# A Mamba block and a mixture of experts on one core: delta's arithmetic moved to 128 partitions by transfers instead of PE transposes, the W_x products and the choosing moved within a round, every table computed in parts

## The chip, the core and the metric

The kernel runs on one core of a Trainium2 chip, in float32 throughout (a few small counting products are bfloat16). The engines of the core have a queue each and run side by side: TensorE (PE) multiplies matrices into PSUM, VectorE (DVE) and ScalarE (ACT) do elementwise work, GpSimd (POOL) does a little of that and issues the indirect transfers (gathers and scatters by a list of rows), and SyncE (SP) issues the other transfers. The metric is the device time of one execution in microseconds, the median over several runs.

## The reference

Two layers, each with a residual sum and a layernorm behind it. T = 4096 tokens of D = 256 values.

```python
xz = x @ W_in                                   # [T, 1024]
conv_in, gated = xz[:, :512], xz[:, 512:]
convolved = silu(causal_conv_of_4_taps(conv_in) + conv_b)
x_dbl = convolved @ W_x                         # [T, 33]
delta = softplus(x_dbl[:, :1])                  # one value per token
Bm, Cm = x_dbl[:, 1:17], x_dbl[:, 17:]
deltaA  = exp(delta * -exp(A_log))              # [T, 16]
deltaBx = delta * Bm * convolved[:, :16]
h_t = deltaA_t * h_(t-1) + deltaBx_t            # along the 4096 tokens
ssm = sum over the 16 states of h_t * Cm_t      # one value per token
x = layernorm(x + ((ssm + convolved * D_param) * silu(gated)) @ W_out)

expert = argmax(x @ Wr.T + br)                  # 8 experts, one per token
y = relu(x @ W1[expert].T + b1[expert]) @ W2[expert].T + b2[expert]
out = layernorm(x + y)
```

## The kernel before

**Two layers in one stream.** The first layer goes in 8 chunks of 512 tokens; its channels lie on partitions and its tokens along the free axis, so that the recurrence over tokens is one scan instruction of DVE. The second layer goes in 32 blocks of 128 tokens of one expert each. A block's rows are gathered from a table in DRAM (`x1d`), into which the first layer scatters its rows by expert. The 2.2 MB of an expert's weights are gathered by POOL into one of three buffers. A block is four *quarters* of PE work: two of `hidden` (lines 617, 626, 628) and two of `close` (line 642).

**What sets the order.** PE's order is exactly that in which the program emits its products. The other engines' orders come from a scheduler, which takes a step marked `@urgent` first. The program emits in rounds: the string `ROUND` lists the steps of a round, each as `name.part:behind`, and in round r the step works on chunk r - behind. So the round with chunk r's projection holds the W_x product of chunk r - 1 (`gauge:1`), its scan (`scan:1`), the gating and output projection of chunk r - 2 (`gate:2`, `project_out:2`), and the ranks of chunk r - 3. `QUARTERS` tells, for each round, how many expert quarters follow each entry; before, they begin in round 7 and the rounds are 12. The quarters left over follow after the last round.

**The steps of a chunk.**
- `project.c` (line 781): two products of 128x512 for each of eight columns of tiles, c = 0 to 3 for the convolution, 4 to 7 for the gate. ACT evicts (796, 798, 800) from three PSUM banks, and takes the silu of a convolved tile (807).
- `taps.c` (752): the three other taps of the convolution, on DVE.
- `gauge` (823): the W_x product with two halves of the channels on two halves of the partitions; ACT copies the result (`pxs`, 828).
- `gauge_out`: four PE transposes (837) bring tokens onto partitions, four tokens to a partition. ACT copies, DVE adds the two halves (`xd`, 847), and the softplus is computed in some fifteen small operations on 128x4 (852 to 871). The result goes into `sr`, delta repeated for 16 states.
- `scan`: four PE transposes (884) bring `sr` back with states on partitions. ACT takes the exponential (886), DVE multiplies (888), scans (890), multiplies by C (896) and splits the product into bfloat16 parts (899).
- `gate`: PE sums over states (`py`, 914), DVE adds the skip and multiplies by the gate (916, 920; one of four tiles on POOL, except in the last two chunks).
- `project_out` (961) multiplies by W_out, with router columns beside it; DVE adds the residual (965), ACT takes squares (968) and normalises (984). `look` and `look_out` (932, 946) give the router's share of x itself.
- `choose` (1000 to 1012) finds each token's expert, `rank` (1022 to 1041) its place, and scatters the rows. `blocks_of` runs `table()`, a generator of small DVE steps that says which rows and weights each block has: early tables after chunks 2, 4 and 5 for 5, 13 and 17 blocks, a final one after the last chunk. Before, an early table is emitted in one piece; the final one is stepped once per quarter. Then `prefetch` issues gathers of rows (532) and weights (561).

SP issues, at the start of a round, the load of the next chunk's x transposed (`xTb`) and of its rows (`xb`), 512 KB each. The constant weights are issued in round 0 by `load_later`. Twelve transposes into an unused bank (229) run at the start, ahead of the first data.

Of the kernel before, what the change touches and what calls it, by code (L numbers as in the profile page):

```python
# [30 lines left out]

# [6 lines left out]
F32 = mybir.dt.float32  # L38
# [8 lines left out]
P = 128  # L47
# [17 lines left out]
WARM = 12  # L65
# [4 lines left out]
SLOTS = 3  # L70
RUN = -(-(SURE - EARLY[6]) // SLOTS)

# [26 lines left out]
RD, RB, RC = 0, 32, 64  # L99
NR = RC + NS  # L100


ROUND = """
    project.0:0 gauge:1 gate:2 project.1:0 taps.0:0 gauge_out:1 taps.1:0 project.2:0
    project.3:0 taps.2:0 project_out.0:2 taps.3:0 rank:3 project_out.1:2 project_out.2:2
    blocks_of:3 look_weights:0 project.4:0 project.5:0 look_out:1 project.6:0 scan:1
    project_out.3:2 choose:2 look:0 project.7:0
"""
ROUNDS = 12

QUARTERS = {
    7: "03001202020010100010001000",
    8: "00100000010110110000000021",
    9: "10001011000101000000001001",
    10: "00000000000110000110000222",
    11: "00010000000000000000000000",
# [6 lines left out]
def mamba_moe(  # L123
# [34 lines left out]
    st = {}  # L158

# [50 lines left out]
    def load_later():  # L210

        nc.sync.dma_start(wx[:, :, 0:XW], W_x.rearrange("(c p) n -> p c n", p=P))
# [15 lines left out]
    for n in range(WARM):  # L228
        nc.tensor.transpose(idle[:, n % 4 * P : (n % 4 + 1) * P], ident, ident)
# [30 lines left out]

    sr = const.tile([P, JT, NR], F32, name="sr")
    nc.gpsimd.memset(sr, 0.0)
# [552 lines left out]
    @urgent  # L815
    def gauge(i):
# [10 lines left out]
        s_["pxs"] = a2.tile([P, TB], F32, tag="pxs", name=f"pxs{i}", bufs=1)  # L827
        nc.scalar.copy(s_["pxs"], px)

    @urgent  # L830
    def gauge_out(i):

        s_ = st[i]
        px = bank("tr", f"pxo{i}", 2)
        for j in range(JT):
            at = slice(j * P, (j + 1) * P)
            nc.tensor.transpose(px[:, at], s_["pxs"][:, at], ident)
        pxv = px.rearrange("p (j h n) -> p j h n", h=P // H, n=H)

        def by_state(a):  # L840
            return a.unsqueeze(2).to_broadcast([P, JT, NS])

        xd = a2.tile([P, JT, XW], F32, tag="xd", name=f"xd{i}", bufs=1)

        parts = a2.tile([P, JT, 2, XW], F32, tag="parts", name=f"parts{i}", bufs=1)
        nc.scalar.copy(parts, pxv[:, :, :, 0:XW])
        nc.vector.tensor_tensor(xd, parts[:, :, 0, :], parts[:, :, 1, :], ALU.add)
        nc.scalar.copy(sr[:, :, RC : RC + NS], xd[:, :, 1 + NS : XW])
        x0 = xd[:, :, 0]

# [300 lines left out]
```

## Time and profile before

| | us |
|---|---|
| median of 3 runs (lowest to highest) | 464.55 (464.51 to 464.59) |
| the profiled execution's own time | 467.2 |
| its span | 465.4 |
| PE busy in the span | 453.4 |
| DVE, ACT, POOL busy | 312.3, 234.4, 159.3 |
| one steady chunk (of rounds 2 to 4) | 25.2 |
| 264 products of the projection (line 781) | 119.0 |
| 864 and 432 products of the expert blocks without extra rows (617, 642) | 102.2, 99.4 |
| 256 products by W_out (961) | 61.9 |
| 64 W_x products (823) | 15.5 |

A profile shows one execution. Times are microseconds (us) within its span. The page's busy times count matmuls with ends that are modelled, so that neighbours overlap: of two groups of products, the difference of their starts tells the cost. In the list of costly groups, `out<-in` are the program's names of the tiles, followed by the shape, the count, the busy time and the mean of one in ns; behind the last bar stands the idle time of the engine just before them, with what ended it. The list of waits names an engine's instruction, the one that released it, and the total, the count and the longest of these waits. In the table of windows the columns are the stretch, its length, each engine's busy time with its instructions in brackets, the granted PE clock, the share of the DMA engines and GB/s. In the timeline a row has the start, the length, the engine and the instruction. In the list of transfers the last number is the median from issue to landing.

### The profile page before, as it was taken

To read this page: it belongs to the slowest core of one execution; us is meant where nothing else is said; L and a number is where in the kernel's file an instruction comes from. 1 tells how busy PE (TensorE), PEld (TensorE's weight loads), DVE (VectorE), ACT (ScalarE), POOL (GpSimd) and SP (SyncE) were. 2 spreads that over 40 slices of the span, in tenths; PEclk is the share of its full clock that TensorE was granted. 3 is DMA by queue.
4 is the path that set the end of the run, shared out by engine and by line. 5 is a ranking of instruction groups with operands and counts; after the bars stand their busy time and mean duration, and the time that the engine had idled before them with its cause. 6 is when DMAs were issued, how large, how long until landed. Compare 5 with 4: busy or idle time off the path is not lost. (4 is left out here: it accounts for less than half of the span.)

```text
span 465.4 us, 7267 instructions
## 1 busy us (share of the span) xinstructions
PE 453.4 (97%) x2496; PEld 339.9 (73%) x2496; DVE 312.3 (67%) x1002; ACT 234.4 (50%) x510; POOL 159.3 (34%) x184
## 2 busy tenths in 40 slices
PE   8999999999999999999999998999999999999994
PEld 6344646465554667876898888999989898989983
DVE  1687969797989869846969368645556565645452
ACT  4787898989879895758553421121212121212120
POOL 3001003214155402352242654435454454434311
PEclk9999999999999999999999999999999999999999
DMA  7501011211229811925646869889986298667400
GB/s 236 176 4 46 0 46 48 89 48 49 92 64 389 353 54 41 365 85 217 247 170 255 283 201 317 328 341 393 360 326 223 58 326 326 227 242 266 179 17 24
DMA packets 20040, 87.38 MB, mean 188 GB/s; under 512 B 4978, under 2 KB 10877, under 8 KB 16418
## 3 DMA queue, kind: packets, MB, share of 16 engines
q0 software_dynamic: 9616, 76.32, 44.2%
q1 hardware_dynamic: 9426, 10.31, 6.7%
q10 hardware_dynamic: 960, 0.27, 0.3%
q8 instruction: 20, 0.33, 0.3%
q14 instruction: 18, 0.15, 0.1%
HBM read 87.16 MB, written 8.77 MB: 206 GB/s over the span
## 5 line engine op out<-in xcount | busy, mean ns | idle before, releaser
L781 PE MATMUL pm<-xTb,win 128*128 128x512 f32 (+1 forms) x264 | 119.0, 589 | 0.0
L617 PEld LDWEIGHTS ph<-xgT,we 128*128 128x128 f32 x864 | 100.4, 192 | 5.4 <-issue 1.8
L617 PE MATMUL ph<-xgT,we 128*128 128x128 f32 x864 | 102.2, 276 | 0.2 <-issue 0.2
L642 PE MATMUL pe<-we,hT 128*128 128x256 f32 x432 | 99.4, 380 | 1.6 <-DVE hT L628 1.2
L642 PEld LDWEIGHTS pe<-we,hT 128*128 128x128 f32 x432 | 79.4, 190 | 13.3 <-DVE hT L628 2.6
L781 PEld LDWEIGHTS pm<-xTb,win 128*128 128x128 f32 x264 | 48.4, 193 | 47.7 <-issue 43.6
L752 DVE SCALAR_TENSOR_TENSOR acc<-xc,cw,acc 128x512 f32<-128x512 f32 x96 | 70.3, 744 | 15.4 <-DMA wx<-in_W_x 8.0
L284 ACT ACTIVATE sdm<-mvm,eps 128x1 f32<-128x1 f32 x32 | 9.4, 294 | 129.9 <-DVE mvm L282 113.1
L961 PE MATMUL po<-wout,sg 128*128 128x265 f32 x256 | 61.9, 389 | 0.7 <-DVE sg L920 0.7
L961 PEld LDWEIGHTS po<-wout,sg 128*128 128x128 f32 x256 | 47.2, 190 | 11.1 <-issue 2.4
L532 POOL DMA_INDIRECT xg<-x1d,tidx x32 | 31.7, 989 | 61.2 <-DMA out<-y,xg 45.6
L561 POOL DMA_INDIRECT we<-in_experts,widx x32 | 34.1, 1064 | 47.7 <-DVE xg L666 10.8
L682 POOL DMA_INDIRECT out<-y,xg x32 | 33.6, 1050 | 42.2 <-DVE y L286 25.5
L628 DVE TENSOR_SCALAR hT<-ph,we 128x128 f32<-128x128 f32 x108 | 31.2, 344 | 24.9 <-PE ph L617 14.9
L1041 POOL DMA_INDIRECT x1d<-x,at x32 | 34.7, 1083 | 29.1 <-DVE q L867 7.4
L666 DVE TENSOR_TENSOR xg<-pe,xg 128x256 f32<-128x256 f32 x32 | 13.5, 423 | 41.9 <-PE pe L642 39.3
L626 ACT ACTIVATE hT<-ph,we 128x128 f32<-128x128 f32 x108 | 30.8, 367 | 13.1 <-PE ph L617 6.7
L965 DVE TENSOR_TENSOR xb<-po,xb 128x265 f32<-128x265 f32 x32 | 13.7, 430 | 26.7 <-PE po L961 25.4
L920 POOL TENSOR_TENSOR sg<-cv,sg 128x512 f32<-128x512 f32 x6 | 7.7, 1278 | 60.4 <-DVE cv L916 60.4
L798 ACT COPY xc<-pm 128x512 f32<-128x512 f32 x32 | 18.6, 581 | 15.4 <-PE pm L781 15.4
L800 ACT ACTIVATE acc<-pm,cb,cw 128x512 f32<-128x512 f32 x32 | 25.1, 784 | 0.2
L968 ACT ACTIVATE x<-xb 128x256 f32<-128x256 f32 x32 | 16.1, 504 | 16.3 <-DVE xb L965 11.9
(221 smaller groups left out, 579.0 us busy)
## 6 DMA issues: line engine op xcount, KB each, us to landing
xb<-in_x SPq DMA_DIRECT2D x8, 512.0 KB, 3.3
xTb<-in_xT SPq DMA_DIRECT2D x7, 512.0 KB, 3.4
win<-in_W_in SPq DMA_DIRECT2D x1, 512.0 KB, 5.9
we<-in_W_outT SPq DMA_DIRECT2D x1, 512.0 KB, 6.1
wout<-in_W_out SPq DMA_DIRECT2D x1, 512.0 KB, 7.0
x1d<-x,at POOLq DMA_INDIRECT x32
we<-in_experts,widx POOLq DMA_INDIRECT x32
xg<-x1d,tidx POOLq DMA_INDIRECT x32
```

Of the source, the lines that this page charges most:

```text
L532: read = nc.gpsimd.indirect_dma_start(out=to.bitcast(I32), out_offset=None, in_=x1d, in_offset=bass.IndirectOffsetOnAxis(ap=at, axis=0),)
L561: nc.gpsimd.indirect_dma_start(out=wes[n][:, :], out_offset=None, in_=experts, in_offset=bass.IndirectOffsetOnAxis(ap=weights[n], axis=0), ...
L617: nc.tensor.matmul(ph[:, n * w : (n + 1) * w], lhsT=we[:, at : at + P], rhs=xgT[:, dc * w : (dc + 1) * w], start=(dc == 0), stop=(dc == DC ...
L626: nc.scalar.activation(hT[:, fc, :], ph[:, n * w : (n + 1) * w], AF.Relu, bias=bias)
L628: last[b] = nc.vector.tensor_scalar(hT[:, fc, :], ph[:, n * w : (n + 1) * w], bias, 0.0, ALU.add, ALU.max)
L642: nc.tensor.matmul(py[:, 0:D], lhsT=hT[:, fc, 0:P], rhs=out_weights(fc), start=(fc == 0), stop=(fc == FC - 1),)
L682: moved = nc.gpsimd.indirect_dma_start(out=out, out_offset=bass.IndirectOffsetOnAxis(ap=at, axis=0), in_=rows, in_offset=None, bounds_chec ...
L752: nc.vector.scalar_tensor_tensor(acc, xc[:, c, k : k + TB], cw[:, c, k : k + 1], acc, ALU.mult, ALU.add)
L781: nc.tensor.matmul(banks[c][:, at], lhsT=win[:, dc, c * P : (c + 1) * P], rhs=xTb[:, dc, at], start=(dc == 0), stop=(dc == DC - 1),)
L800: evicted = nc.scalar.activation(acc, pm, AF.Identity, scale=cw[:, c, KC - 1 : KC], bias=cb[:, c : c + 1])
L961: nc.tensor.matmul(po[:, 0 : D + NM], lhsT=sg[:, c, j * P : (j + 1) * P], rhs=wout[:, c, :], start=(c == 0), stop=(c == CC - 1),)
L1041: moved = nc.gpsimd.indirect_dma_start(out=x1d, out_offset=bass.IndirectOffsetOnAxis(ap=at[:, j : j + 1], axis=0), in_=x1s[i % X1S][:, j, ...
```

## The change

- *Delta.* The two groups of four transposes go. The columns of W_x are laid out anew, B first, then delta's column repeated 16 times, then C; this takes three transfers and a copy on DVE. `gauge` adds the two halves on DVE (`half`, `bcd`), which leaves 16 equal rows of 512 pre-activations on partitions 16 to 31, and a transfer brings these 16x512 onto 128 partitions by 64 (`x0`). The new step `delta` does the softplus there, on 128x64 instead of 128x4, and a second transfer brings it back to 16x512 (`wide`). `scan` works from these without PE.
- *Order of a round.* `gauge` moves from the next round's start to the end of the chunk's own, `look` to the next round, `delta` and `scan` follow; `choose` is listed just before `gauge`. `gauge`, `scan`, `look_out`, `rank` and `blocks_of` lose their mark `@urgent`; `delta` has one.
- *Tables.* Early tables become generators that are stepped once per entry of a round, with the prefetch at their end; the final one starts 8 quarters later.
- *The rest.* `gate`'s last tile of the last two chunks goes to POOL. The warm-up is 8 float32 products on a constant that DVE sets, instead of 12 transposes. The quarters are placed anew, from round 6 on, and the rounds are 17.

```diff
...
 
 
 from contextlib import ExitStack
+from itertools import chain
 
 import concourse.bass as bass
 import concourse.tile as tile
...
 
 SURE = 32
 
-WARM = 12
+WARM = 8
 
 AHEAD = 2
 
 
 SLOTS = 3
+
+WAIT = 8
 RUN = -(-(SURE - EARLY[6]) // SLOTS)
...
 OC = OB + FC
 WROW = OC + D
 
-RD, RB, RC = 0, 32, 64
+RB, RD, RC = 0, 16, 32
 NR = RC + NS
+SEG = P // NS
 
 
 ROUND = """
-    project.0:0 gauge:1 gate:2 project.1:0 taps.0:0 gauge_out:1 taps.1:0 project.2:0
-    project.3:0 taps.2:0 project_out.0:2 taps.3:0 rank:3 project_out.1:2 project_out.2:2
-    blocks_of:3 look_weights:0 project.4:0 project.5:0 look_out:1 project.6:0 scan:1
-    project_out.3:2 choose:2 look:0 project.7:0
+    project.0:0 gate:2 taps.0:0 look:1 look_weights:0 project.1:0 project.2:0 taps.2:0
+    taps.1:0 project_out.0:2 project.3:0 project_out.1:2 taps.3:0 look_out:1 project.4:0
+    rank:3 delta:1 project.5:0 project_out.2:2 project.6:0 blocks_of:3 scan:1
+    project_out.3:2 choose:2 gauge:0 project.7:0
 """
-ROUNDS = 12
+ROUNDS = 17
 
 QUARTERS = {
-    7: "03001202020010100010001000",
-    8: "00100000010110110000000021",
-    9: "10001011000101000000001001",
-    10: "00000000000110000110000222",
-    11: "00010000000000000000000000",
+    6: "00000000000000000001001001",
+    7: "00201001000001100000000230",
+    8: "20110002001000000000000010",
+    9: "12001000000100100300001010",
+    10: "00000010001100000000001000",
+    12: "00011010000000010000000000",
+    16: "00000001000000000000000000",
 }
 
 LOG_SERIES = (0.33333338, 0.19999444, 0.14308298, 0.1071537, 0.1214478)
...
 
     st = {}
 
+    stir = const.tile([P, P], F32, name="stir")
+    nc.vector.memset(stir, 1.0)
+
     def load(i):
 
         xTb = a2.tile([P, DC, TB], F32, tag="xTb", name=f"xTb{i}")
...
 
     def load_later():
 
-        nc.sync.dma_start(wx[:, :, 0:XW], W_x.rearrange("(c p) n -> p c n", p=P))
+        for to, n, at in ((RB, NS, 1), (RC, NS, 1 + NS), (NR, 1, 0)):
+            nc.sync.dma_start(
+                wx[:, :, to : to + n], W_x[:, at : at + n].rearrange("(c p) n -> p c n", p=P)
+            )
+        nc.vector.tensor_copy(
+            wx[:, :, RD : RD + NS], wx[:, :, NR : NR + 1].to_broadcast([P, CC, NS])
+        )
         nc.sync.dma_start(al, A_log)
         nc.sync.dma_start(dp, D_param)
         nc.sync.dma_start(woutT, W_outT.rearrange("(c p) n -> p c n", p=P))
...
 
     idle = bank("tr", "idle", 2)
     for n in range(WARM):
-        nc.tensor.transpose(idle[:, n % 4 * P : (n % 4 + 1) * P], ident, ident)
+        nc.tensor.matmul(
+            idle[:, n % 4 * P : (n % 4 + 1) * P], lhsT=stir, rhs=stir, start=True, stop=True
+        )
 
     def iota(shape, pattern, base, channel, name, dtype=F32):
         t = const.tile(shape, dtype, name=name)
...
         trib, oneb, pattern=[[1, P]], compare_op=ALU.is_gt, fill=0.0, base=0,
         channel_multiplier=-1,
     )
-
-    sr = const.tile([P, JT, NR], F32, name="sr")
-    nc.gpsimd.memset(sr, 0.0)
 
     parts_ = const.tile([P, TB], F32, name="parts_")
     nc.gpsimd.memset(parts_, 0.0)
...
             )
             nc.gpsimd.tensor_copy(after[:, :, 0 : KC - 1], xc[:, :, TB : TB + KC - 1])
 
-    @urgent
     def gauge(i):
...
                 px[g : g + H, :], lhsT=wx[:, c, :], rhs=cv[:, c, :],
                 start=(c < 2), stop=(c >= CC - 2), tile_position=(0, g),
             )
-        s_["pxs"] = a2.tile([P, TB], F32, tag="pxs", name=f"pxs{i}", bufs=1)
-        nc.scalar.copy(s_["pxs"], px)
+        half = a2.tile([P, TB], F32, tag="half", name=f"half{i}", bufs=1)[0:NR, :]
+        nc.scalar.copy(half, px[H : H + NR, :])
+        bcd = s_["bcd"] = a2.tile([P, TB], F32, tag="bcd", name=f"bcd{i}", bufs=2)
+        nc.vector.tensor_tensor(bcd[0:NR, :], px[0:NR, :], half, ALU.add)
+        x0 = s_["x0"] = a2.tile([P, TB // SEG], F32, tag="x0", name=f"x0{i}")
+        nc.sync.dma_start(x0, bcd[RD : RD + NS, :])
 
     @urgent
-    def gauge_out(i):
-
-        s_ = st[i]
-        px = bank("tr", f"pxo{i}", 2)
-        for j in range(JT):
-            at = slice(j * P, (j + 1) * P)
-            nc.tensor.transpose(px[:, at], s_["pxs"][:, at], ident)
-        pxv = px.rearrange("p (j h n) -> p j h n", h=P // H, n=H)
-
-        def by_state(a):
-            return a.unsqueeze(2).to_broadcast([P, JT, NS])
-
-        xd = a2.tile([P, JT, XW], F32, tag="xd", name=f"xd{i}", bufs=1)
-
-        parts = a2.tile([P, JT, 2, XW], F32, tag="parts", name=f"parts{i}", bufs=1)
-        nc.scalar.copy(parts, pxv[:, :, :, 0:XW])
-        nc.vector.tensor_tensor(xd, parts[:, :, 0, :], parts[:, :, 1, :], ALU.add)
-        nc.scalar.copy(sr[:, :, RC : RC + NS], xd[:, :, 1 + NS : XW])
-        x0 = xd[:, :, 0]
-
-        e = a2.tile([P, JT], F32, tag="e", name=f"e{i}")
+    def delta(i):
+
+        x0 = st[i]["x0"]
+
+        def small(tag):
+            return a2.tile([P, TB // SEG], F32, tag=tag, name=f"{tag}{i}", bufs=1)
+
+        e = small("e")
         nc.vector.scalar_tensor_tensor(e, x0, -1.0, x0, ALU.mult, ALU.min)
         grown = nc.scalar.activation(e, e, AF.Exp)
         if i == 0:
             with tc.issue_after(grown.ins):
                 nc.scalar.activation(nega, al, AF.Exp)
             nc.vector.tensor_scalar(nega, nega, -1.0, None, ALU.mult)
-        s = a2.tile([P, JT], F32, tag="s", name=f"s{i}")
+        s = small("s")
         nc.vector.tensor_scalar(s, e, 2.0, None, ALU.add)
         nc.vector.reciprocal(s, s)
         nc.vector.tensor_tensor(s, s, e, ALU.mult)
-        w = a2.tile([P, JT], F32, tag="w", name=f"w{i}")
+        w = small("w")
         nc.vector.tensor_tensor(w, s, s, ALU.mult)
-        q = a2.tile([P, JT], F32, tag="q", name=f"q{i}")
+        q = small("q")
         nc.vector.tensor_scalar(q, w, LOG_SERIES[-1], None, ALU.mult)
         for a in LOG_SERIES[-2::-1]:
             nc.vector.scalar_tensor_tensor(q, q, a, w, ALU.add, ALU.mult)
         nc.vector.scalar_tensor_tensor(q, q, 1.0, s, ALU.add, ALU.mult)
-        delta = a2.tile([P, JT], F32, tag="delta", name=f"delta{i}")
-        nc.vector.tensor_scalar(delta, x0, 0.0, None, ALU.max)
-        nc.vector.scalar_tensor_tensor(
-            sr[:, :, RD : RD + NS], by_state(q), 2.0, by_state(delta), ALU.mult, ALU.add
-        )
-        nc.vector.tensor_tensor(
-            sr[:, :, RB : RB + NS], xd[:, :, 1 : 1 + NS], sr[:, :, RD : RD + NS], ALU.mult
-        )
-
-    @urgent
+        nc.vector.tensor_scalar(x0, x0, 0.0, None, ALU.max)
+        nc.vector.scalar_tensor_tensor(q, q, 2.0, x0, ALU.mult, ALU.add)
+        wide = st[i]["wide"] = a2.tile([P, TB], F32, tag="wide", name=f"wide{i}", bufs=1)
+        nc.sync.dma_start(wide[0:NS, :], q)
+
     def scan(i):
-        s_, cv = st[i], st[i]["cv"]
-        hbefore = st[i - 1]["h"] if i else None
-        pt = bank("tr", f"pt{i}", 2)
-        for j in range(JT):
-            nc.tensor.transpose(pt[0:NR, j * P : (j + 1) * P], sr[:, j, :], ident)
-        dA = a2.tile([NS, TB], F32, tag="dA", name=f"dA{i}", bufs=1)
-        nc.scalar.activation(dA, pt[RD : RD + NS, :], AF.Exp, scale=nega)
-        dBx = a2.tile([NS, TB], F32, tag="dBx", name=f"dBx{i}", bufs=1)
-        nc.vector.tensor_tensor(dBx, pt[RB : RB + NS, :], cv[0:NS, 0, :], ALU.mult)
-        h = a2.tile([NS, TB], F32, tag="h", name=f"h{i}")
+        s_, cv, bcd, wide = st[i], st[i]["cv"], st[i]["bcd"], st[i]["wide"]
+        low, up = slice(0, NS), slice(RC, RC + NS)
+        dBx = a2.tile([P, TB], F32, tag="half", name=f"dBx{i}", bufs=1)
+        nc.vector.tensor_tensor(dBx[low, :], bcd[RB : RB + NS, :], cv[low, 0, :], ALU.mult)
+        nc.scalar.activation(wide[up, :], wide[low, :], AF.Exp, scale=nega)
+        nc.vector.tensor_tensor(dBx[up, :], dBx[low, :], wide[low, :], ALU.mult)
+        h = s_["h"] = a2.tile([P, TB], F32, tag="h", name=f"h{i}")
         nc.vector.tensor_tensor_scan(
-            h, dA, dBx, 0.0 if hbefore is None else hbefore[:, TB - 1 : TB],
+            h[up, :], wide[up, :], dBx[up, :], st[i - 1]["h"][up, TB - 1 : TB] if i else 0.0,
             ALU.mult, ALU.add,
         )
-
-        s_["h"] = h
-        nc.vector.tensor_tensor(parts_[0:NS, :], pt[RC : RC + NS, :], h, ALU.mult)
+        nc.vector.tensor_tensor(parts_[low, :], bcd[up, :], h[up, :], ALU.mult)
         for n in range(2):
             this = slice(n * Q, n * Q + NS)
             nc.vector.tensor_tensor(
...
             nc.vector.scalar_tensor_tensor(
                 cv[:, c, :], cv[:, c, :], dp[:, c : c + 1], py, ALU.mult, ALU.add
             )
-            eng = nc.vector if c in ((0, 1, 2, 3) if i >= NB - 2 else (1, 2, 3)) else nc.gpsimd
+            eng = nc.vector if c in ((0, 1, 2) if i >= NB - 2 else (1, 2, 3)) else nc.gpsimd
             eng.tensor_tensor(sg[:, c, :], cv[:, c, :], sg[:, c, :], ALU.mult)
 
     rxs = {}
...
         rxs[i] = a2.tile([P, n], F32, tag="rx", name=f"rx{i}", bufs=3)
         nc.scalar.copy(rxs[i], prx[:, 0:n])
 
-    @urgent
     def look_out(i):
 
         pf = bank("tr", f"pf{i}", 2)
...
         nc.vector.tensor_tensor(earlier[:, i + 1, :], earlier[:, i, :], here, ALU.add)
         st[i]["oh"], st[i]["best"] = oh, best
 
-    @urgent
     def rank(i):
         oh, best = st[i]["oh"], st[i]["best"]
...
                 tc.declare_no_dep(moved.ins, group=group, reason="tokens have places of their own")
             tc.add_to_no_dep_group(f"placed{i}", moved.ins)
 
-    @urgent
+    early = []
+
+    def table_ahead(done, columns):
+        yield from table(done, EARLY[columns] - done, columns, True)
+        prefetch(current)
+
     def blocks_of(i):
 
         done = len(weights)
         if i + 1 in EARLY:
-            for _ in table(done, EARLY[i + 1] - done, i + 1, True):
-                pass
+            early.append(table_ahead(done, i + 1))
         elif i == NB - 1:
-            pieces.append(table(done, NSB - done, NB, False))
+            pieces.append(chain((None,) * WAIT, table(done, NSB - done, NB, False)))
         prefetch(current)
 
     def have(i):
...
 
 
     steps = dict(
-        project=project, taps=taps, gauge=gauge, gauge_out=gauge_out, scan=scan, gate=gate,
+        project=project, taps=taps, gauge=gauge, delta=delta, scan=scan, gate=gate,
         look=look, look_out=look_out, project_out=project_out, choose=choose, rank=rank,
         blocks_of=blocks_of,
     )
...
                     look("w")
             elif have(i):
                 steps[name](i, *(int(n) for n in at))
+            for t in early:
+                next(t, None)
             if r == 1 and name == "look_out":
                 look_out("w")
             if r == 0 and entry == "project.2:0":
```

## The prediction

> **What bounds the kernel now.** First the page's busy times and the list of what TensorE (PE) waited for.
>
> ```profile
> PE 453.4 (97%) x2496; PEld 339.9 (73%) x2496; DVE 312.3 (67%) x1002; ACT 234.4 (50%) x510; POOL 159.3 (34%) x184
> PEclk9999999999999999999999999999999999999999
> ...
> PE idle L229 <- POOL ident masks.py:199: 1.6, 1, 1.6
> PE pe L642 <- DVE hT L628: 1.2, 3, 0.6
> PE po L961 <- DVE sg L920: 0.7, 1, 0.7
> PE pr L1022 <- DVE oh L1009: 0.4, 1, 0.4
> PE py L914 <- DVE parts__143 L899: 0.4, 1, 0.4
> ```
>
> The reader is to see that PE works all through at the full granted clock and waited only some 5 us. So a PE instruction less is time less, as long as nothing new makes PE wait. Next the busy times by window, one steady chunk to a row (us of the stretch, then PE, weight loads, DVE, ACT, POOL):
>
> ```profile
> 66.78:91.96 25.18, 25.18 (x98) 13.77 (x97) 21.61 (x59) 22.50 (x43) 7.14 (x7) 1.00 0.18 63
> 91.96:117.14 25.18, 25.18 (x98) 13.77 (x97) 21.60 (x59) 22.48 (x43) 7.15 (x7) 1.00 0.19 64
> ```
>
> A chunk takes 25.18 us, all of it PE; VectorE (DVE) has 3.6 us to spare and ScalarE (ACT) 2.7. That is all the cover there is. Last the timeline: PE at the two groups of transposes, and the transfers of one loaded stretch.
>
> ```profile
> 110.61 0.60 PE L884 MATMUL pt<-ident,sr 128*80 128x128 f32 x4
> 111.05 1.96 PE L961 MATMUL po<-wout,sg 128*128 128x265 f32 x8
> ...
> 120.96 0.60 PE L837 MATMUL pxo<-ident,pxs 128*128 128x128 f32 x4
> 121.39 3.60 PE L781 MATMUL pm<-xTb,win 128*128 128x512 f32 x8
> ...
> xb<-in_x SPq DMA_DIRECT2D x8, 512.0 KB, 3.3
> xTb<-in_xT SPq DMA_DIRECT2D x1, 512.0 KB, 10.7
> ```
>
> Ends of matmuls are modelled, so I price by the next start: four transposes cost 0.44 us. A 512 KB load lands in 3.3 us alone, but in 10.7 when it is issued 3.3 us after an expert's weights.
>
> **The change part by part.**
>
> *Transposes.* Both groups go, for 8 chunks: 16 x 0.44 = -7.0 us on PE.
>
> *Steady chunks (rounds 2 to 5).* PE's list is then 25.18 - 0.88 = 24.3 us. DVE: out go xd (0.29, in the pipeline 0.21) and the two sr operations (0.13 each); fifteen operations go from 128x4 (0.15, 0.075 to the next start) to 128x64 (0.22, 0.13, as the sr ones are now), +0.8; in come the sum into bcd and a second product into dBx, each like the 0.68 us row of dBx. Together 0.8 + 0.72 + 0.72 - 0.47 = +1.8, so 23.4 of 24.3 us. ACT loses 0.38 and 0.25. It fits, but the order has to fit too. I count from the start of a round's first project product (1.71 us each; po 1.79; py 0.24; prx 0.76 and px 2.09 with the switch to them):
> - The last taps end near 18.9, project.6 at 18.7. ACT: sg 0.5, the last silu 0.53, table load 1.28, exp over wide 0.68, so 22.0. DVE: scan 1.27, three operations of 0.72, so 25.4. py is due at 24.3 + 1.7 = 26.0. Slack 0.6 us.
> - bcd then ends 1.8 into the next round. The transfer to x0 leaves; DVE does dBx and three gate operations first and wants x0 at 4.5. So 2.7 us are free. The nearest rows: an xTb load issued at 20.73 put its first packet at 21.7 and its last at 23.65 and landed at 3.2; without the 1.9 us of packets that leaves 1.3, plus some 0.5 for 128 rows of 256 B: 1.8 to 2.0. Upper bound 3.3, the 512 KB row. I take 2.0: hidden.
> - The transfer into wide leaves near 15.5 and is wanted near 19: 3.5 free, hidden at 2.0 and at 3.3.
> - rank wants oh at 13.4; choosing among the taps has it at 12.2. Slack 1.2. The last sg of the gate is ready at 7.4, its product is due at 7.5.
> So +0.04 a chunk, +0.2 in all; at 3.3 us per transfer +0.6 a chunk, +2.4; below it cannot go, PE's list being the floor.
>
> [...]
>
> *Opening.* W_x comes in three pieces; SP issues two more (0.37 to 0.5 us each) ahead of al, dp, W_outT, W_out, br and the rows of x. None of these is wanted before 22 us. But DVE's copy of the delta column waits for the last piece and stands ahead of chunk 0's second tap. Before, that tap ran at 11.1; the one piece was issued at 6.15 and took 5.3. Two issues later, it lands near 12.1; the copy 0.3: taps 1.3 later, to 20.1 instead of 19.08. The W_x product now stands in its own round, so PE arrives at 18.35 and its second pair at 19.3, but the last silu is ready at 20.8: +1.5. Then bcd, transfer, exp and chain push chunk 1's taps to 38.1; its product waits 0.5, and py of chunk 0 1.1, where it waited 0.4 before. Sum +2.7 - 0.4 = +2.3. Bounds: 0 (pieces land by 11.1 and the taps keep pace) and +4 (the piece takes 7.0, as W_out did).
>
> *Round 6.* The first expert's load is issued about 2.2 us before the round, x0 of chunk 5 2 us into it. Before, the load left at 137.51, xTb at 140.81, and xTb's first packet came at 144.6, 7.1 after the load's issue. The same here gives 4.9 into the round, landing 5.7, against 4.5 wanted: with the round's own wait +1.3. Bounds 0 and +6.7 (7.4 us more, as xTb had, less the 0.7 free). Behind x0 on SP stand the next xTb, rows of x and the transfer into wide. They delay exp over wide to about 23, ahead of the last silu on ACT; PE has the first expert products (3.6 us) there, which cover it.
>
> [...]
>
> *Rounds 7 and 8.* Expert quarters (1.8 us of PE each) lengthen a round to over 40 us while DVE's share grows less: waits of some us are covered. 0; bounds 0 and +2.
>
> *Tables in parts, gate's last part to POOL, later final table.* They spread DVE's table work. PE's waits behind DVE between 225 and 286 us were 0.69 + 0.44 + 0.16 + 0.41 + 0.61 = 2.3 us; I take -0.6, bounds -2.3 and +2 (new such waits, since all quarters are replaced). POOL's gate product takes 1.28 against 0.68, and its queue holds row scatters and weight loads (about 1 us per issue); po of chunks 6 and 7 stands quarters later, which hides it.
>
> *Start.* Warm-up passes 12 to 16 at 0.2 us from an earlier memset: 2.4 becomes 3.2, beginning 0.6 earlier. The first real product waits for data at 4.35. 0; bounds -0.2 and +0.3.
>
> **Sum.** -7.0 + 0.2 + 2.3 + 1.3 + 0 - 0.6 + 0 = -3.8 us. The profiled execution took 467.2 (span 465.4 and 1.8 around it): 463.4. The median is 2.65 below the profiled one: 464.55 - 3.8 = 460.75, I say 460.7.
>
> **Rivals.**
> - *The transfers become the wait.* x0 is late every round: DVE's in-order queue then holds back gate and taps, ACT's exp the eviction that frees project's third bank. Each us over 2.7 costs a us in rounds 1 to 5. It undoes the forecast from 3.8/5 = 0.76 over, 3.5 us a transfer. For it: 10.7 us under load, and only 0.7 to spare. Against: the 3.3 us of sixteen times the bytes. At 4 us: +6.5, 467.2, slower.
> - *DVE becomes the bound.* 23.4 of 24.3 us, with chains across engines; if each handover costs 0.1 more than I read, chunks stay at 25.18 and 4 x 0.88 = 3.5 is lost: 464.2, no change.
> - *More comes.* No opening wait, table waits gone, round 6 free: -7.0 + 0.2 - 2.3 = -9.1, 455.5; half of that is likelier, 457.
>
> **How the numbers follow.** Forecast 0.52, transfers 0.22, DVE 0.12, more 0.14. Changes within 0.2% (0.9 us) cannot be told from none. Faster: 0.52 + 0.14 and a little of DVE's case, 0.68; same 0.10; slower 0.22. The range goes from 456.5 (most of the last case) to 466.5 (a transfer of 3.9 us, or round 6 at its bound): about 0.8.
>
> **What would show it.** In the changed profile: no pxo or pt rows; steady rounds of 24.3 us; DVE near 23.4 in them; x0 landing about 2 us after issue; PE waits for silu at px of chunk 0 (1.5) and for parts at py of chunk 0 (1.1); 1.3 in round 6; fewer waits for hT. Wrong if DVE idles behind the x0 transfer in steady rounds, if PE waits for sg or for a bank there, or if quarters starve for weights.

## The result and the profile after

The changed kernel takes 465.68 us (median of 22 executions, 464.46 to 466.83), the kernel before 464.56 on the same chip: a ratio of 1.0025, interval 1.0016 to 1.0033. It is a little slower, where 3.8 us less had been forecast. Chips differ by some microseconds (464.4 to 467.7 for before), so below a time is compared only with before's on its own chip.

The page of the profiled execution (465.82 us, span 464.0): busy times, then PE's busy tenths and its granted clock in 40 slices of 11.6 us.

```profile
PE 450.1 (97%) x2435; PEld 337.5 (73%) x2436; DVE 324.5 (70%) x1002; ACT 230.8 (50%) x493; POOL 161.2 (35%) x185
...
PE   9999999999996999999999999999999999999994
...
PEclk9999999999999799999999999999999999999998
```

Apart from the last one, all but two slices look like before's. In the thirteenth (139 to 151 us) PE is busy for 6 tenths; in the fourteenth (151 to 162 us) the clock is 7 tenths. The list of what PE waited for names it:

```profile
PE po L954 <- DVE sg L914: 5.0, 1, 5.0
PE idle L244 <- DVE stir L167: 1.1, 1, 1.1
PE py L908 <- DVE parts__139 L893: 0.7, 1, 0.7
```

There is one wait of 5.0 us, and the waits for hT that before had are gone. The timeline around it, several engines together (start, length, engine, instruction, idle time before it and its releaser):

```profile
140.44 1.28 POOL L575 DMA_INDIRECT we<-in_experts,widx  x1 [0.30 <-DVE parts__139 L890]
142.63 0.58 SPq L845 DMA_DIRECT2D x<-bcd  x1
150.93 0.23 DVE L856 SCALAR_TENSOR_TENSOR e<-x 128x64 f32<-128x64 f32 x1 [5.64 <-DMA x<-bcd]
151.19 0.26 ACT L857 ACTIVATE e<-e 128x64 f32<-128x64 f32 x1 [5.11 <-DVE e L856]
151.81 3.32 PE L954 MATMUL po<-wout,sg 128*128 128x265 f32 x6 [5.02 <-DVE sg L914]
```

This is round 6. The first expert load (2.2 MB) leaves at 140.44 and x0 of chunk 5 at 142.63. The 32 KB of x0 land 8.3 us later. DVE stands before `e`, the first reader, for 5.6 us, with the gate products that PE needs queued behind it; ACT stands before its exponential with the evictions behind it. PE has run dry. The table of windows of 2 us (columns as before, the clock third from the right) shows what follows:

```profile
146.00:148.00 2.00, 0.79 (x3) 0.19 (x1) 0.00 (x0) 0.07 (x1) 1.44 (x2) 1.00 0.99 422
148.00:150.00 2.00, 0.00 (x0) 0.00 (x0) 0.00 (x0) 0.00 (x0) 1.64 (x2) 1.00 0.93 360
150.00:152.00 2.00, 0.19 (x1) 0.19 (x2) 1.07 (x3) 0.81 (x2) 1.39 (x3) 0.53 1.07 368
152.00:154.00 2.00, 2.00 (x5) 1.11 (x5) 2.00 (x6) 2.00 (x6) 1.24 (x1) 0.50 1.18 411
154.00:156.00 2.00, 2.00 (x4) 1.27 (x5) 2.00 (x8) 0.69 (x2) 0.00 (x0) 0.50 0.99 410
156.00:158.00 2.00, 2.00 (x5) 0.96 (x5) 2.00 (x9) 0.16 (x1) 0.00 (x0) 0.77 0.98 419
```

After the gap PE has half its clock for 5.1 us; a projection pass there takes 0.85 us from its start to the next one's, instead of 0.43. Summing what each pass takes over its usual time gives 5.2 us for the gap and 2.8 for the slow passes, 8.0 us in one place. The steady rounds before it did what was forecast, by the table of windows from one W_x product to the next:

```profile
86.86:111.48 24.62, 24.62 (x89) 12.93 (x89) 22.45 (x58) 22.14 (x41) 6.49 (x7) 1.00 0.21 69
111.48:136.24 24.76, 24.76 (x90) 12.96 (x89) 23.39 (x65) 22.24 (x41) 6.61 (x7) 1.00 0.21 69
```

They take 24.6 and 24.8 us instead of 25.18, all of it PE, at full clock, with DVE at 22.5 to 23.4.

### The profile page after: what moved, and what is told of

Read it like the earlier page. It is cut to its first block, busy times and chain, and to the rows that moved or that the text cites. A ratio compares the mean times of both kernels' runs of the same rounds, so it can differ in the third digit from the quotient of the medians.

```text
span 464.0 us, 7169 instructions
## 1 busy us (share of the span) xinstructions
PE 450.1 (97%) x2435; PEld 337.5 (73%) x2436; DVE 324.5 (70%) x1002; ACT 230.8 (50%) x493; POOL 161.2 (35%) x185
## 4 chain that ended last, share of the span: by engine, by line
PE 77%; DMA 10%; DVE 7%; ACT 3%; issue 2%; POOLq 0%; SPq 0%; ACTq 0%; POOL 0%; DVEq 0%
PE ph L631 22%; PE pe L656 21%; PE pm L795 17%; PE po L954 11%; DMA we<-in_experts,widx 6%; DVE acc L766 3%; PE px L836 2%; DMA x<-bcd 2%; PE pg L601 1%; PE pf L667 1%; DMA cw<-in_conv_w 1%; DMA wx<-in_W_x 1%; PE prx L926 1%; DVE parts__139 L893 1%; ACT L883 1%
## 5 line engine op out<-in xcount | busy, mean ns | idle before, releaser
L795 PE MATMUL pm<-xTb,win 128*128 128x512 f32 (+1 forms) x264 | 120.5, 595 | 0.0
L954 PE MATMUL po<-wout,sg 128*128 128x265 f32 x256 | 64.9, 396 | 5.0 <-DVE sg L914 5.0
L954 PEld LDWEIGHTS po<-wout,sg 128*128 128x128 f32 x256 | 48.4, 193 | 24.0 <-issue 9.3
L1033 POOL DMA_INDIRECT x1d<-x,at x32 | 33.7, 1053 | 39.0 <-DVE at L1030 21.2
L642 DVE TENSOR_SCALAR hT<-ph,we 128x128 f32<-128x128 f32 x108 | 30.9, 342 | 22.6 <-PE ph L631 22.5
L914 POOL TENSOR_TENSOR sg<-cv,sg 128x512 f32<-128x512 f32 x8 | 10.9, 1368 | 41.0 <-DVE cv L910 40.9
L827 POOL COPY xc<-xc 128x12 f32<-128x12 f32 x7 | 3.2, 461 | 61.8 <-ACT xc L812 61.8
L961 ACT ACTIVATE x<-xb 128x256 f32<-128x256 f32 x32 | 16.1, 503 | 16.5 <-DVE xb L958 16.4
```

What stands on the lines that cost most here:

```text
L642: last[b] = nc.vector.tensor_scalar(hT[:, fc, :], ph[:, n * w : (n + 1) * w], bias, 0.0, ALU.add, ALU.max)
L795: nc.tensor.matmul(banks[c][:, at], lhsT=win[:, dc, c * P : (c + 1) * P], rhs=xTb[:, dc, at], start=(dc == 0), stop=(dc == DC - 1),)
L954: nc.tensor.matmul(po[:, 0 : D + NM], lhsT=sg[:, c, j * P : (j + 1) * P], rhs=wout[:, c, :], start=(c == 0), stop=(c == CC - 1),)
L1033: moved = nc.gpsimd.indirect_dma_start(out=x1d, out_offset=bass.IndirectOffsetOnAxis(ap=at[:, j : j + 1], axis=0), in_=x1s[i % X1S][:, j, ...
```

## The experiments

Theory A: an expert load that leaves shortly ahead of x0 holds x0 back until it is through; everything else follows from that. The rivals: the orders of DVE and ACT are bad anyway (B); the clock falls for another reason than the gap (C); SP's queue is what delays x0.

### The first loads behind the gate product

```diff
         yield from table(done, EARLY[columns] - done, columns, True)
+        if done == 0:
+            yield
+            with tc.issue_after(anchors["gate", 4]):   # POOL's product of gate(4)
+                prefetch(current)
         prefetch(current)
```

> Edit: the gathers of the first early table (four of rows, then the three expert loads) are queued on POOL behind its gate product of round 6, so that x0 of chunk 5 leaves ahead of them. Nothing else moves.
> Theory A (the load of 2.2 MB that was issued 2.2 us before x0 holds its last packet back, DVE stands in order behind it, PE runs dry for 5.0 us and then gets half its clock for 5.4 us, which costs another 2.8): x0 lands in about 2.1 us instead of 8.3, PE does not wait at its first product by W_out in round 6, the clock stays at 1.00 there, and the time falls by 5.2 + 2.8 = 8.0 us, to about 458 against 465.7. Up to 1.5 us may come back, because the transfer into wide now leaves among the loads.
> Rival B (the products of DVE and ACT are simply in a worse order in round 6, whatever x0 does): PE still waits for sg, and the time falls by less than 2 us.
> Rival C (the low clock comes from the load of the chip, not from the gap): the gap goes, the half clock stays; the time falls by 5 us.

Measured: 466.1 to 467.3 us in six executions and 470.8 to 477.4 in six others, before 467.7 on that chip; the ratio, 0.9995 (0.9969 to 1.0022), is that of the first group and the 470.8 together. The 8 us that A expected did not come: the first group lies 2.6 us below the 469.04 of the next run, which has the full wait in round 6 on the same chip. The one profile is of the slowest execution (477.44). In it x0 of chunk 5 lands in 2.1 us, PE waits 0.5 us in that place and the clock stays at 1.00 there:

```profile
PE po L956 <- DVE sg L914: 0.5, 1, 0.5
```

So B and C fall for round 6. But the same thing happens in two other places. From the timeline, first `wide` of chunk 5, then x0 of chunk 7:

```profile
167.44 0.72 ACT L883 ACTIVATE wide<-wide,nega 16x512 f32<-16x512 f32 x1 [7.82 <-DMA wide<-q]
...
215.26 1.01 POOL L575 DMA_INDIRECT we<-in_experts,widx  x1 [0.30 <-ACT half L841]
215.71 0.58 SPq L845 DMA_DIRECT2D x<-bcd  x1
225.55 0.23 DVE L856 SCALAR_TENSOR_TENSOR e<-x 128x64 f32<-128x64 f32 x1 [7.17 <-DMA x<-bcd]
226.38 4.63 PE L656 MATMUL pe<-we,hT 128*128 128x256 f32 x10 [5.47 <-ACT hT L640]
```

`wide`, issued at 156.36, is caught by the three loads that now leave at 151.3 to 155.1; ACT stands 7.8 us for it, PE 1.2 us for a silu queued behind it, and another 1.5 us for the first load itself, which leaves later than in the changed kernel. And behind a load that leaves 0.45 us ahead of it x0 of chunk 7 takes 9.8 us; that costs another 5.5 us of PE and 5.6 us at half clock. In the changed kernel's profile this x0 left 1.3 us ahead of that load and went through. The second group of times is what one would expect if the two change places from execution to execution; no execution of the first group has a profile, so that is argued, not shown, and what the first group still lost stays open.

### x0 of chunk 5 from ACT's queue

```diff
-        nc.sync.dma_start(x0, bcd[RD : RD + NS, :])
+        (nc.scalar if i == 5 else nc.sync).dma_start(x0, bcd[RD : RD + NS, :])
```

> Edit: x0 of chunk 5 alone is issued from ACT's queue instead of SP's. It tells whether x0 was late because of the queue it was in or because of the DMA engines behind the queues.
> If the engines are what it waits for (each of the 16 works off the packets of the expert load that it has, 8 of 17 KB at 0.65 us): x0 still lands 7 to 8 us after its issue, PE still waits 4 to 5 us, and the time stays within 1 us of 465.7.
> If SP's queue was the reason: x0 lands in 2 to 3 us, no wait, the time about 458.

Measured: 469.04 us, ratio 1.0038 (1.0021 to 1.0055); the unchanged kernel had 1.0025 and 1.0046 on two other chips. The timeline:

```profile
140.68 1.28 POOL L575 DMA_INDIRECT we<-in_experts,widx  x1 [0.30 <-DVE parts__139 L890]
142.87 0.65 ACTq L845 DMA_DIRECT2D x<-bcd  x1
151.21 0.23 DVE L856 SCALAR_TENSOR_TENSOR e<-x 128x64 f32<-128x64 f32 x1 [3.07 <-DMA x<-bcd]
152.09 1.25 PE L954 MATMUL po<-wout,sg 128*128 128x265 f32 x2 [4.16 <-DVE sg L914]
```

The queue is not the reason: x0 takes 8.3 us from ACT's queue as well, and PE waits 4.2. The trace's packets agree: the load's 128 rows of 17 KB (0.65 us in the median, eight to an engine on average) run from 142.6 to 150.1, and x0's 128 pieces of 256 B, 0.018 us each, from 147.0 to 150.6, the last five of them after the load's last row had ended. The trace does not name the engine of a packet, so in what order an engine took the two is not shown.

### Products that nobody reads, into the gap

```diff
+        if i == 4 and j == 0:
+            spare_ = bank("tr", "filler", 2)
+            for n in range(FILL):                      # FILL = 6
+                nc.tensor.matmul(
+                    spare_, lhsT=stir, rhs=st[5]["cv"][:, 0, :], start=True, stop=True
+                )
         po = bank("o", f"po{i}_{j}")
```

> Edit: six float32 products of 128x512, whose result nobody reads (0.86 us each by the rows of the projection, 5.1 together), are put ahead of the first products by W_out in round 6, into the 5.2 us in which PE waits for x0's followers. No wait is taken away.
> Theory A (the low clock follows from PE standing still): the clock stays at 1.00 in the 6 us behind the gap, PE's products there take their usual time, and the kernel is faster by about 2.8 us although it does more: about 463.0 against 465.7.
> Rival C (the low clock has another reason): the clock still falls to 0.5, and the time stays or grows.

Measured: 473.29 us, ratio 1.0131 (1.0103 to 1.016); on the same chip the kernel of the section above had 1.0038. So it is some 4 us slower, not 2.8 faster. The table of windows and the list of PE's waits:

```profile
150.00:152.00 2.00, 2.00 (x7) 0.95 (x5) 0.82 (x3) 0.56 (x2) 1.69 (x2) 1.00 1.07 379
152.00:154.00 2.00, 1.38 (x6) 0.64 (x4) 2.00 (x7) 2.00 (x5) 1.19 (x1) 1.00 1.08 365
...
162.00:164.00 2.00, 0.00 (x0) 0.00 (x0) 2.00 (x6) 1.30 (x6) 0.00 (x0) 1.00 0.89 373
164.00:166.00 2.00, 1.97 (x9) 0.97 (x9) 1.83 (x5) 1.97 (x4) 0.00 (x0) 0.81 0.07 18
166.00:168.00 2.00, 2.00 (x6) 1.17 (x5) 1.87 (x5) 1.97 (x3) 0.80 (x1) 0.50 0.00 0
```
```profile
PE pr L1022 <- ACT rparts L948: 3.5, 1, 3.5
```

With the gap filled the clock stays at 1.00 from 146 to 164 us, so C falls: the half clock in this place came with the gap of PE. But the time was not to be had. DVE and ACT had lost 5 us each behind x0 all the same. In the run before, where PE came back late and at half clock, it met no further wait of 0.5 us or more before 252 us. Here it came back at full clock, ran into ACT 9 us later, stood for 3.5 us and got half its clock then. ACT itself had stood 2.5 us for DVE, which worked without a pause from 151.2 to 165.4. The 2.8 us were no separate cost that could be saved while x0 was late.

### The first three loads spread over rounds 6 and 7

```diff
+            for n_, r_, at_ in ((1, 6, "rank"), (2, 7, "gate")):
+                if (r, name) == (r_, at_):
+                    hold.discard(n_)                   # loads 1 and 2 are held until here
+                    with tc.issue_after(anchors[at_, i]):
+                        prefetch(current)
```

> Edit: as in the first run, and besides the three first expert loads are spread: the first right behind POOL's gate product of round 6, the second behind the row scatters of that round (about 163 us), the third behind the gate product of round 7, so that each leaves just after one of the small transfers and is through before the next.
> Theory A: x0 of chunks 5 and 6 and the transfers into wide of rounds 6 and 7 all land in 2 to 3 us; no PE wait and full clock in round 6; faster than the first run by what its transfer into wide loses there (0 to 1.5 us): 457 to 458.
> Rival: PE waits for the second or third load instead, then 1 to 5 us of waits for we appear in round 7, and it is no faster than the first run.

Measured: 470.23 us, ratio 1.0055 (1.0037 to 1.0073). x0 of chunk 5 lands in time again, but now load 0 is queued on POOL ahead of the gathers of the first rows, which come through behind it, and PE waits for those:

```profile
PE pg L602 <- DMA xg<-x1d,tidx: 4.9, 1, 4.9
```

The order of loads and rows was badly chosen by me; the run says nothing against A, only that small gathers came late behind a load in their own queue too: the first of them left 1.8 us behind load 0, at 146.94, and PE's first product from it starts 10.3 us later, at 157.19. Nor did the transfers of chunk 6 land in the 2 to 3 us expected: x0 took 6.0 us behind a load that left 3.9 us ahead of it, and `wide` 8.4. DVE stood 4.1 us and ACT 3.4 us for them, but PE did not wait. So lateness alone does not set the price; in round 7 PE had expert quarters to do meanwhile.

### Before and after again, on one chip, beside a kernel with guards

In the guarded kernel POOL reads a column of x0 (chunks 5 to 7) and of `wide` (chunk 5), which it can do only once they have landed (it stood 4.7 us for `wide`), and the next load is queued behind that read. The rows of the first two blocks go ahead of load 0.

```diff
+    def guard(name, i, a):
+        n = len(anchors) % 16
+        anchors[name, i] = nc.gpsimd.tensor_copy(seen[0 : a.shape[0], n : n + 1], a[:, 0:1]).ins
...
+                with tc.issue_after(anchors["x0", 7]) if n == 5 else nullcontext():   # load 5, behind x0 of chunk 7
...
         nc.sync.dma_start(x0, bcd[RD : RD + NS, :])
+        if i >= 5:
+            guard("x0", i, x0)
+        if i == 6:
+            hold.discard(2)                            # load 2 leaves behind x0 of chunk 6
+            with tc.issue_after(anchors["x0", 6]):
+                prefetch(current)
...
         nc.sync.dma_start(wide[0:NS, :], q)
+        if i == 5:
+            guard("wide", i, wide[0:NS, :])
+            hold.discard(1)                            # load 1 leaves behind wide of chunk 5
+            with tc.issue_after(anchors["wide", 5]):
+                prefetch(current)
...
+        if done == 0:
+            prefetch(current, (0, 1), False)           # rows of blocks 0 and 1, no load
+            yield
+            with tc.issue_after(anchors["gate", 4]), tc.issue_after(anchors["x0", 5]):
+                prefetch(current, ())                  # load 0 alone
+            with tc.issue_after(anchors["load", 0]):
+                prefetch(current)
```

> The kernel before, unchanged, for a profile on the same chip as the following three: the chip of the first four runs took 467.7 us for it, the one of the first comparison 464.6. No theory is at stake; its busy times and waits are the base of the sums.

> The changed kernel, unchanged, on the same chip as the kernel with guards.
> Theory A: x0 of chunk 5 lands 7 to 9 us after its issue, PE waits 4 to 5.5 us and then has half its clock for 3 to 5.5 us; ratio to before 1.000 to 1.005. x0 of chunk 7 is issued within 1 to 2 us of another expert load, so that in single executions it can be caught as well, and the times may scatter.

> Edit: POOL reads one column of x0 (chunks 5 to 7) and of wide (chunk 5) once each has landed, and the expert load that would have left just ahead of it is queued behind that read on POOL; the rows of the first two blocks are gathered ahead of the first load. So no load of weights can be in front of one of these four transfers.
> Theory A: x0 and wide land 2 to 3 us after issue in rounds 6 to 8, PE never waits more than 2 us between 100 and 300 us, the clock stays at 1.00 there, and the time is 5 to 8 us below the unguarded kernel's: ratio to before about 0.985 to 0.99 (458 to 460 where before takes 464.6).
> Rival (other waits take the place: the loads now come too late for blocks 1 and 2, or DVE's order is what lacks): waits for we or hT of 2 us and more appear and the ratio stays above 0.993.

Measured: before 464.47 us, after 466.46, ratio 1.0046 (1.0031 to 1.0061); with guards 459.85, ratio 0.9908 (0.9873 to 0.9944). PE's wait in the unguarded kernel on this chip, then the guarded kernel's timeline, its list of PE's waits and two of its windows:

```profile
PE po L954 <- DVE sg L914: 5.9, 1, 5.9
```

```profile
142.95 0.58 SPq L852 DMA_DIRECT2D x<-bcd  x1
145.54 0.99 DVE L869 SCALAR_TENSOR_TENSOR e<-x 128x64 f32<-128x64 f32 x1
146.73 1.36 POOL L582 DMA_INDIRECT we<-in_experts,widx  x1
149.27 0.71 PE L974 MATMUL po<-wout,sg 128*128 128x265 f32 x2 [0.77 <-DVE sg L932]
```
```profile
PE idle L244 <- DVE stir L167: 1.1, 1, 1.1
PE po L974 <- DVE sg L932: 0.8, 1, 0.8
PE py L926 <- DVE parts__139 L911: 0.7, 1, 0.7
```
```profile
148.00:150.00 2.00, 1.24 (x5) 0.75 (x5) 2.00 (x7) 2.00 (x4) 1.39 (x3) 1.00 1.16 361
150.00:152.00 2.00, 2.00 (x7) 0.98 (x7) 2.00 (x7) 0.34 (x2) 0.62 (x1) 1.00 0.92 360
```

x0's last piece runs at 144.8, and the load leaves after it. The wait of 5.9 us that the unguarded kernel has in this place on this chip is 0.8, no other has come, and the clock stays at 1.00. The guards, with the order that they give the loads and rows, turn a loss of 2.0 us into a gain of 4.6. These 6.6 us lie within the 5 to 8 that A expected (the ratio lies just above its 0.985 to 0.99), and this version beats both kernels. Apart from POOL's four tiny reads nothing but the order of loads, rows and small transfers was changed. What A expected of the later transfers did not all come: x0 of chunks 6 and 7 took 3.4 us, and `wide` of chunk 7, which has no guard, 6.7 us behind a load that left 4.2 us ahead of it. ACT stood 1.1 us for that one, and PE did not wait.

The three profiles of this chip, with PE's time by groups of products, each product from its start to the next one's (the waits in front of a group's products lie in the group before or in it; the small groups are left out, so that the rows do not sum up to the last one):

| us | before | after | with guards |
|---|---|---|---|
| start: until the first real product | 4.4 | 4.7 | 4.7 |
| transposes of delta | 7.1 | 0 | 0 |
| projection | 113.9 | 114.9 | 114.4 |
| W_out | 59.4 | 66.5 | 60.2 |
| W_x | 15.4 | 16.3 | 16.5 |
| experts: first layer | 118.0 | 118.3 | 118.3 |
| experts: second layer, 128 rows | 111.9 | 111.3 | 111.3 |
| start of the last product | 455.5 | 457.2 | 450.6 |

Between before and after the 7.1 us are saved and 7.1 come back under W_out alone, with another us in the projection. In round 6 the gap is 6.0 us and the slow passes cost 2.5, so 8.5 us: 7.8 of them lie under W_out and 0.7 under the projection. The table's row for W_out shows only 7.1, since before has a wait of 0.9 there, at 225 us, that after has lost.

### x0 through two transfers in the steady rounds

```diff
+        if 1 <= i <= 4:
+            first_ = a2.tile([P, TB // SEG], F32, tag="first", name=f"first{i}")
+            nc.sync.dma_start(first_, bcd[RD : RD + NS, :])
+            nc.sync.dma_start(x0, first_)
+        else:
+            nc.sync.dma_start(x0, bcd[RD : RD + NS, :])
```

> Edit: in chunks 1 to 4, where no expert's weights are in flight, x0 goes through two transfers, one after the other, the second of them behind the next load of xTb in SP's queue. It doubles the disputed cost in the steady rounds alone.
> Forecast's reading (2.7 us are free between x0's issue and its first reader, each us over that costs a us of PE): x0 is ready some 5 us after the first issue instead of 2.1, DVE waits about 2 us for it in rounds 2 to 5, and the steady period grows from 24.6 to 26 to 27 us, +6 to +10 us in all.
> Rival (DVE's and ACT's queues have room and take it up): period below 25, less than 2 us in all.

Measured: 471.71 us (two executions), ratio 1.0153 against 1.0046; the profiled one is 4.0 us longer than after's. Most of it is one wait, for chunk 1's sum over states, with 3.4 us at half clock behind it. Then the first readers of x0 of chunks 3 and 4:

```profile
71.10 0.39 PE L913 MATMUL py<-parts__139,oneb 128*128 128x512 bf16 x1 [3.01 <-DVE parts__139 L898]
...
102.28 0.23 DVE L861 SCALAR_TENSOR_TENSOR e<-x 128x64 f32<-128x64 f32 x1
126.92 0.22 DVE L861 SCALAR_TENSOR_TENSOR e<-x 128x64 f32<-128x64 f32 x1
```

In the two rounds after it the period from one W_x product to the next is 24.7 and 24.75 us, as without the second transfer. The price per round was wrong: the scheduler knows of two transfers and puts the reader of x0 later in DVE's order (at 102.3 and 126.9 us, 5.3 us behind the first issue instead of 2.7, with no wait in front of it). In these rounds a delay that the schedule was made for costs nothing; for chunk 1 the wait above came with it. One that the schedule did not know of, as in round 6, kept DVE standing for 5.6 us, and PE with it for 5.0.

### The smaller parts, on the guarded kernel

```diff
 # in one piece: the early tables' steps at once and urgent, as before
-        yield from table(done, EARLY[columns] - done, columns, True)
+        with tc.high_priority():
+            steps_ = sum(1 for _ in table(done, EARLY[columns] - done, columns, True))
+        yield from (None,) * steps_
 # final table at once
-WAIT = 8
+WAIT = 0
 # gate's last part on DVE
-            eng = nc.vector if c in ((0, 1, 2) if i >= NB - 2 else (1, 2, 3)) else nc.gpsimd
+            eng = nc.vector if c in ((0, 1, 2, 3) if i >= NB - 2 else (1, 2, 3)) else nc.gpsimd
```

> The kernel with guards once more, as the base of the three following on whatever chip they get. Theory A: ratio to before 0.988 to 0.993, no wait of PE over 2 us between 100 and 300 us, clock at 1.00 there.

> Edit on the kernel with guards: the steps of the early tables are emitted at once and marked urgent, as before; their prefetch stays where it is. It prices tables in parts by itself.
> The forecast's term was -0.6 us for all of tables, late final table and gate (bounds -2.3 and +2): in one piece some 0.3 us slower, within 1 us.
> Rival (the DVE work of a table ahead of scan and gate lets PE run dry): waits for sg or parts of 1 us and more in rounds 6 to 8, 2 to 4 us slower.

> Edit on the kernel with guards: the final table starts at once (WAIT 0 instead of 8 quarters). It prices the later start.
> Forecast: part of the -0.6 us; 0 to 0.5 us slower, as new waits of PE behind DVE between 225 and 290 us.
> Rival: the final table has slack in both places, no difference beyond the scatter.

> Edit on the kernel with guards: the fourth gate product of the last two chunks is on DVE again, as before, instead of on POOL.
> Forecast: nothing, since po of these chunks stands quarters later; within 0.5 us.
> Rival: POOL's 1.3 us and its queue of transfers make PE wait for sg, then this is 0.5 to 1.5 us faster.

Measured, before 464.35: the guarded kernel 459.49, ratio 0.9900 (0.9882 to 0.9917), the second time that it gains 1%. In one piece 460.12 (0.9913), no later start 460.10 (0.9918), gate on DVE 459.65 (0.9897). With four executions each and a scatter of about a us, the first two may cost 0.6 us, the third nothing; all are far too small to explain the result.

## Why the prediction was wrong

It forecast 460.7 and got 465.68, inside its range but on the other side of no change. The range's upper end, 466.5, stood for late transfers or for round 6 at its bound, and round 6 went past its bound.

- **Round 6, forecast +1.3 with a bound of +6.7, measured +8.0 (8.5 on the other chip): this is the step that failed.** It named the right transfer and the right load, and took the right row, the xTb load that left 3.3 us behind an expert load. Its size was wrong in three places. It used that transfer's *first* packet, 7.1 us after the load's issue. In the changed kernel x0's first packet came at 6.2, but its *last* at 9.8: its last pieces ran only when the load's last row had ended, at 149.9 us. It took the load to leave 2.2 us ahead of the round; it left 0.6 us into it, since the four row scatters of `rank` stood in front of it on POOL until 140.1, so x0 left 2.2 us behind the load instead of 4.2, when the load's first rows were only starting (142.4). And it priced a wait of PE by its length alone; the half clock behind it added 2.8 us.
- **The sign of the rival with late transfers was right, its shape was not.** Its x0 was to be late in every round, at 3.5 us and more. Over the eight chunks it lands in 2.6 us in the median, and outside rounds 1 and 6 DVE waits 0.4 us for it in all; it holds DVE up by 5.6 us in round 6, and by 2.5 us in the opening. The doubled transfer shows that the price of a us per us and round was wrong as well, at least for chunks 3 and 4.
- **x0 by itself, 2.0 us forecast: right.** In rounds 3, 4 and 7 it lands in 2.1 us. Its first piece runs 1.3 us after the issue and its 128 pieces of 256 B take 0.54 us, where the forecast put some 0.5, an estimate that no row of before shows. In round 6 the first piece ran 4.0 us after the issue and the last five when the load was through. But 13 of its 128 pieces had run by 147.5 us, when 19 of the load's 128 rows were still to start, so x0 did not have to wait for the whole load. Why its pieces ran when they did is not shown.
- **Transposes, -7.0: right**, 7.1 us in the same-chip table.
- **Steady rounds, 24.3 us forecast, 24.4 to 24.8 measured**: about 0.7 us more in all than the +0.2, whose 0.04 a chunk the prediction took from no row (its +2.4 also counts four rounds where the +0.2 counts five). DVE came to 22.5 to 23.4 us, against 23.4.
- **Opening, +2.3 forecast, about +1.5 measured**: PE stands 1.1 us in the W_x product of chunk 0 and 0.9 in front of the first sum over states, where before had 0.5. The places were right; the copy of delta's column ran at 11.8, a little sooner than taken.
- **Tables, late waits and gate, -0.6 forecast, about -1.5 measured on one chip: right in sign.** The waits behind DVE that the first profile of before showed between 260 and 286 us are missing in its second, which took 464.48 as the median does: they belonged to that one execution, and with 2.6 us they make up the 2.65 by which it lay over the median. In the second, waits of 1.7 us remain (at 225, 245 and 248 us), of which after has 0.2.
- **Rounds 7 and 8, 0: right, in round 8 only by luck.** That round 7 covers some us is what the spread loads show, where DVE stood 4.1 us there and PE did not wait. But in round 8 x0 of chunk 7 leaves 1.3 us ahead of a load; in the first experiment it left 0.45 us behind one, and PE stood for 5.5 us.

With round 6 cleared by guards the kernel gains 4.6 to 4.9 us; the other terms of the forecast sum to -5.1. That the two agree is partly chance: the opening and the tables came out 0.8 and 0.9 us better than forecast, the steady rounds 0.7 worse, and in round 6 a wait of 0.8 us is left.

## To carry to other kernels

In this kernel 32 KB that left 0.45 to 4.2 us behind a load of 2.2 MB took 6.0 to 9.8 us, from SP's queue as from ACT's, and 2.0 and 3.2 when they left 7.0 and 7.2 us behind it, so look for what is still in flight, on other queues too, when a small transfer leaves, and price it by the last packet. If it must be on time, let the issuer of the large transfers wait for it: four tiny reads on that engine, and the order they imposed, were worth 1.4% here. By my estimate a gap of PE of 3.0 to 5.9 us cost 1.3 to 1.6 times its length, worked out as the gap and half of the slow time behind it, as the figures below give them.

## What the runs showed of the hardware

- Behind gaps of PE of 3.0 to 5.9 us its granted clock was 0.50 for a while. In the changed kernel it was 0.50 for 6.83 us, from 150.11 to 156.94; the gap of 5.0 us ended at 151.81, so 5.1 of the slow time lay behind it. With the loads spread, windows of 2 us give 6.8 us around the gap of 4.9. They give 3.4 us behind the gaps of 4.2 (x0 from ACT's queue), 3.5 (filled gap) and 5.1 (x0 through two transfers, round 6), beginning 0 to 1.2 us after PE was back. What sets the length is not shown: gaps of 5.0 and 5.1 us had different ones. Products were slow as well behind the gaps of 3.0 (x0 through two transfers, chunk 1: eight projection passes in 5.2 us instead of 3.4), 5.5 (first experiment: 5.6 us at half clock behind it) and 5.9 us (the unguarded kernel beside the guarded one). Behind waits of 1.5 and 1.2 us, at 161 and 170 us of the first experiment, the clock stayed at 1.00. What the passes took over their usual time was 1.8 us behind the gap of 3.5, 2.8 and 2.5 behind those of 5.0 and 5.9. I had not weighed it: the longest wait of PE in before's profile is 1.6 us, at the start.
- In the changed kernel's rounds 3 to 5 each transfer of 32 KB whose landing is on record, x0 and `wide`, landed in 2.0 to 2.2 us. x0 took 8.1 to 9.8 us when it left 0.45 to 2.2 us behind 2.2 MB, on SP's queue and on ACT's alike. It came shortly after the large one: by the packets, x0 of chunk 5 ended 0.4 us after the load's last row in the changed kernel (150.3 us after 149.9) and 0.5 from ACT's queue (150.6 after 150.1); by the landings, `wide` of chunk 7, which left 7.2 us behind a load in the changed kernel and still took 3.2, came 0.5 us after it (228.5 after 228.0).
